# Two scan steps and two attention groups in one loop turn of a conv, state-space, attention and expert kernel

## The chip, the core and the metric

The kernel runs on one core of a Trainium2 chip. The metric is device microseconds of one execution. The kernel before takes 5496.23 us, the median of 3 runs (5489.41 to 5500.91).

The engines are named as in the profile: PE is TensorE (matrix products, accumulated in PSUM banks), DVE is VectorE, ACT is ScalarE, POOL is GpSimd, and SP is the queue that issues nearly all transfers. Each works through its own instructions strictly in program order.

## The reference

An image batch `x` (4, 128, 64, 64) goes through two layers. Layer 0 is group norm, a depthwise convolution with a pointwise one, and a state-space scan (Mamba) on four channel chunks. Layer 1 is attention over 4096 tokens with 4 heads of 32, then the two best of 8 experts. The change touches the scan and the attention:

```python
# scan, for every channel d, state n (16 of them), step t
h = dA_t * h + dBu_t              # dA = exp(delta * A), dBu = delta * B * xin
y = jnp.einsum('bdn,bn->bd', h, C_t)

# attention
scores = jnp.einsum('bhnd,bhmd->bhnm', q, k) * scale
att = jax.nn.softmax(scores, axis=-1)
out = jnp.einsum('bhnm,bhmd->bhnd', att, v)
```

## The kernel before, in words

**Tiling.** An image of 4096 positions is cut into 8 blocks of 512 (`BLK`). The scan of a block runs for two chunk pairs `p`, each on 128 partitions, and for 16 states `n`. One (batch, block, pair, state) is a *unit*; there are 4 x 8 x 2 x 16 = 1024. Attention is cut into *groups*: for one head and 1024 queries, two tiles of 128 keys. There are 1024 groups.

**The loop.** The order of instructions is written out by hand. The main loop takes one turn, a *slot*, per unit, and goes on afterwards until the remaining groups and expert work are done. In a slot:

- SP fetches the B and C rows of the unit three slots ahead from DRAM (`rows<-bcd`, broadcast over the partitions, 4 buffers).
- ACT copies the last column of the unit before into `states`, and computes `da`, the exponential of the decay, for the unit two slots ahead.
- PE computes the scores of the next group: four matmuls into two PSUM tiles `sc` of two banks each. The pool of `sc` has two buffers, so one group fills it. ACT turns them into `pT` by two exponentials.
- DVE runs the unit: `h` = B row times `du`, then the scan (`tensor_tensor_scan`) with the saved state as start value, then `hc` = C row times `h`.
- From `ALONE` (unit 128) on, POOL adds the `hc` of every odd state to that of the even one, and PE adds four transposes of the sum to the PSUM tile `y`, from two slots after the odd state on. Before `ALONE`, PE adds each `hc` by a full matmul with the identity one slot later. After the last state, `y` is copied out, turned back by four transposes, and goes on (`summed_up`).
- PE computes the weighted sums `av` of the group of the slot before (`weighted`, four matmuls in two passes each). When a sum is complete, ACT copies it from PSUM (`avs`), which has one buffer.

**Side work.** All else (norms, convolution, projections, softplus, routing, experts) is written as generators in two lanes, X and Y, of which `advance` runs one stage at a time: each lane has one call marked second and one marked first per slot. Stages hand on from one engine to another: PE writes a PSUM tile, DVE or ACT reads it in a later call. In a slot the calls come after the scan step and the score matmuls: X second, Y first, then the transposes of `y`, Y second, then `weighted`, X first. `until` runs stages early where a unit's inputs aren't ready.

**Transfers.** `send` puts a transfer in a list that `flush` issues at the start of a later slot. Keys and values of the next part are fetched three groups before a part ends.

Of the kernel before, what the change touches and what calls it, by code (L numbers as in the profile page):

```python
# [9 lines left out]
F32 = mybir.dt.float32  # L10
F32R = mybir.dt.float32r
# [25 lines left out]
def conv_mamba_attn_moe_kernel(ctx: ExitStack, tc: tile.TileContext, t: dict):  # L37
# [450 lines left out]
        return ps_work.tile(shape or [P, BLK], F32, tag=f"work{lane}", name=f"ps_{lane}")  # L488

    def tmp(lane, name, shape=None):  # L490
        return side.tile(shape or [P, BLK], F32, tag=f"tmp{lane}", name=name, bufs=4)

    def transposed(lane, src):
        ps = work(lane)
# [184 lines left out]
    def inputs(b, i, p):  # L679

        xn, pairs = xn_of[b, i], pairs_of[b, i]
        r = slice(DI * p, DI * p + DI)
        while held:
            yield
            yield
        held.add("in")
        ps = work("Y")
        summed(ps, [(inxc[:, j, :], pairs[:, p, 2 * j : 2 * j + BLK]) for j in range(2)])
        pz = work("X")
        mm(pz, inz[r, :], xn[r, 3 : 3 + BLK])  # L690
        yield
        xin = mix.tile([P, BLK], F32, name="xin", bufs=2)
        scalar.activation(xin, ps, AF.Silu, bias=cb)
        zs = mix.tile([P, BLK], F32, name="zs", bufs=4)
        scalar.activation(zs, pz, AF.Silu)
        yield

        pb = work("X")
        mm(pb[0:DI, :], wbc, xin)
        ps = work("Y")  # L700
        mm(ps, wdt, xin)
        yield
        held.clear()
        bc = tmp("Y", "bc")[0:DI, :]
        scalar.copy(bc, pb[0:DI, :])
        bcd = dram.tile([2, NST, 2 * BLK], F32, name="bcd", bufs=4)
        send(bcd.rearrange("c n (k q) -> (c n k) q", k=2), bc)

        e = tmp("Y", "e")
        scalar.activation(e, ps, AF.Abs, bias=dtb)  # L710
        scalar.activation(e, e, AF.Exp, scale=-1.0)
        ln = tmp("Y", "ln")
        scalar.activation(ln, e, AF.Ln, bias=1.0)
        delta = mix.tile([P, BLK], F32, name="delta", bufs=2)
        scalar.activation(delta, ps, AF.Relu, bias=dtb)
        yield
        yield

        du = mix.tile([P, BLK], F32, name="du", bufs=2)
        lost = du  # L720
        gpsimd.tensor_scalar(lost, e, 1.0, -1.0, ALU.add, ALU.add)
        gpsimd.tensor_sub(lost, e, lost)
        gpsimd.tensor_add(ln, ln, lost)
        gpsimd.tensor_add(delta, delta, ln)
        gpsimd.tensor_mul(du, delta, xin)
        in_of[b, i, p] = xin, zs, delta, du, bcd
        done.add(("in", b, i, p))
        yield

    states = [mix.tile([P, 2, NST], F32, name=f"state{k}") for k in range(2)]  # L730

    def fetched(b, i, p, n):

        bcd = in_of[b, i, p][4]
        w = mix.tile([P, 2, BLK], F32, name="rows", bufs=4)
        sync.dma_start(
            out=w.rearrange("p k q -> p (k q)"),
            in_=bcd[:, n, :][None].to_broadcast([DI, 2, 2 * BLK]),
        )
        return w  # L740

    def decayed(b, i, p, n):
        da = mix.tile([P, BLK], F32, name="da", bufs=3)
        scalar.activation(da, in_of[b, i, p][2], AF.Exp, scale=amat[:, n : n + 1])
        return da

    def scan(b, i, p, n, w, da):

        du = in_of[b, i, p][3]
        h = mix.tile([P, BLK], F32, name="h", bufs=3)  # L750
        vector.tensor_mul(h, w[:, 0, :], du)
        vector.tensor_tensor_scan(
            out=h, data0=da, data1=h, initial=0.0 if i == 0 else states[b % 2][:, p, n : n + 1],
            op0=ALU.mult, op1=ALU.add,
        )
        hc = mix.tile([P, BLK], F32, name="hc", bufs=5)
        vector.tensor_mul(hc, w[:, 1, :], h)
        return h, hc

    def scanned(b, i, p, y):  # L760
        xin, zs, delta, du, bcd = in_of.pop((b, i, p))
# [28 lines left out]
    def closed(b, i):  # L790
# [58 lines left out]
        for d, w, bias in ((kd, wkn, bkn), (qd, wqn, bqn)):  # L849
            ps = work("X")  # L850
            mm(ps, w, xa)
            yield
            hi = side.tile([P, BLK], F32R, name="hi", bufs=2)
            vector.tensor_scalar(hi, ps, bias, None, ALU.add)
            lo = side.tile([P, BLK], F32R, name="lo", bufs=2)
            vector.scalar_tensor_tensor(
                lo, ps, bias, hi.bitcast(F32), ALU.add, ALU.subtract
            )
            for half, w in enumerate((hi, lo)):
                w = w.bitcast(F32)  # L860
                if len(d.shape) == 4:
                    send(d[:, :, half, sj], w[:, None, :].to_broadcast([P, 2, BLK]))
                else:
# [54 lines left out]
    def attention(b):  # L918
# [25 lines left out]
        for at, part in enumerate(parts):  # L944
# [9 lines left out]
            for g in range(0, NT * n, STEP):  # L954
# [5 lines left out]
                if g >= NT * n - 3 * STEP and ahead is None and at + 1 < len(parts):  # L960
                    nxt = parts[at + 1]
                    if ready(b, nxt):
                        ahead = load(nxt, qs if nxt[:2] == (q, h) and not nxt[5] else None)
                pTs = []
                for j in range(g, g + STEP):
                    sc = ps_sc.tile([P, 2, BLK], F32, name="sc")
                    for u in range(2):
# [1 line left out]
                            sc[:, u, :], ks[:, j * P : (j + 1) * P],  # L969
                            qs[:, u * BLK : (u + 1) * BLK],  # L970
                        )
                    pT = att.tile([P, 2, BLK], F32, name="pT", bufs=4)
                    scalar.activation(pT, sc, AF.Exp, scale=ATT_SCALE)
                    pTs.append((v[:, j // NT, j % NT, :], pT))
                yield (
                    b, q, h, pTs, first and g == 0, last and g + STEP == NT * n, prev, final,
                )

    sums, partial, total, inverse, later = [None], {}, {}, {}, deque()

    def weighted(group):
        b, q, h, pTs, first, last, prev, final = group
# [175 lines left out]
    def advance(lane, second):  # L1158
# [3 lines left out]
        while True:  # L1162
            if lane not in running:

                tasks = lanes[lane] if lanes[lane] or slot < len(units) else lanes["X"]
                if not tasks or not all(k in done for k in tasks[0][2]):
                    return False

                if (
                    tasks[0][0][0] == "out" and slot < len(units) + 4  # L1170
                    and not 2 <= slot % (2 * NST) < NST + 2
                ):
                    return False
# [62 lines left out]
        left.clear()  # L1236

    groups = attention_groups()
    units = [(b, i, p, n) for b, i in blocks for p in range(2) for n in range(NST)]

    ALONE = NB // 2 * 2 * NST
    rows, decays, old, due, closing = {}, {}, None, deque(), deque()
    even, y_of, waiting, slot = None, {}, None, 0
    while slot < len(units) or due or closing or waiting or left or later or lanes["X"] or running:
        flush()

        for ahead in range(slot if slot == 0 else slot + 3, min(slot + 4, len(units))):
            until(("in", *units[ahead][:3]))
            rows[ahead] = fetched(*units[ahead])
        if old:  # L1250
            (b, i, p, n), h = old
            if i < NB - 1:
                scalar.copy(states[b % 2][:, p, n : n + 1], h[:, BLK - 1 : BLK])
            old = None
        for ahead in range(slot if slot == 0 else slot + 2, min(slot + 3, len(units))):
            decays[ahead] = decayed(*units[ahead])
        group = next(groups, None)
        if slot < len(units):
            unit = units[slot]
            h, hc = scan(*unit, rows.pop(slot), decays.pop(slot))  # L1260
            old = unit, h
            b, i, p, n = unit

            if slot < ALONE:
                due.append((slot + 1, unit, hc, n == 0))
            elif n % 2 == 0:
                even = hc
            else:
                gpsimd.tensor_add(even, even, hc)
                due.append((slot + 2, unit, even, n == 1))  # L1270
        advance("X", True)
        advance("Y", False)
        while closing and closing[0][0] <= slot:
            turned_back(*closing.popleft()[1:])
        while due and due[0][0] <= slot:
            at, unit, term, first = due.popleft()
            b, i, p, n = unit
            if first:
                y_of[b, i, p] = ps_y.tile([P, BLK], F32, name="y")
            y, ends = y_of[b, i, p], n == NST - 1  # L1280
            if at <= ALONE:
                mm(y, ident, term, first, ends)
                if ends:
                    summed_up(b, i, p, y_of.pop((b, i, p)))
            else:
                turned_on(y, term, first, ends)
                if ends:
                    yT = mix.tile([P, BLK], F32, name="yT")
                    scalar.copy(yT, y_of.pop((b, i, p)))
                    closing.append((slot + 1, b, i, p, yT))  # L1290
        advance("Y", True)
        if waiting:
            weighted(waiting)
        waiting = group
        advance("X", False)
        while later and later[0][0] <= slot:
            next(later.popleft()[1])
# [28 lines left out]
def _laid_out(i):  # L1326
# [15 lines left out]
    z = np.zeros((P, P), np.float32)  # L1342
    inx, inz = z.copy(), z.copy()
    wout = np.zeros((P, 2, P), np.float32)
    wbc = np.zeros((P, 2, NST, 2), np.float32)
    xdt, dtT = np.zeros((4, P), np.float32), np.zeros((4, P), np.float32)
    for c in range(2):
        d = slice(c, P, 2)
# [3 lines left out]
            inz[s, d] = c0["in_proj_w"][DI:].T  # L1352
            wout[d, p, s] = c0["out_proj_w"].T

        wbc[d, c] = c0["x_proj_w"][2:].reshape(2, NST, DI).transpose(2, 1, 0)
        xdt[2 * c : 2 * c + 2, d] = c0["x_proj_w"][:2]
        dtT[2 * c : 2 * c + 2, d] = c0["dt_proj_w"].T

# [53 lines left out]
```

## Time and profile before

| | us |
|---|---|
| median of 3 runs | 5496.23 |
| the profiled execution | 5490.03 |
| its span, first to last instruction | 5488.3 |
| ACT `pT`, 2048 exponentials | 1983.1 |
| PE `av`, 8192 passes | 2022.7 |
| DVE scans with a start value, 896 | 1364.1 |
| PE `sc`, 4096 | 1333.3 |
| DVE `hc`, 1024 | 882.4 |
| DVE `h` (multiplication), 1024 | 843.3 |
| ACT `da`, 1024 | 751.2 |
| POOL `hc`, 448 additions | 677.6 |
| ACT table loads, 320 | 410.6 |

The busy time of a group counts moments in which one of its instructions runs; the groups of one engine follow each other, and those of different engines overlap. All recorded instructions carry line 445, that of a helper that orders them, so groups are told apart by their tiles: `h<-rows,du` is the multiplication, `h<-da,state,h` the scan, `hc<-rows,h` the reading on DVE, `hc<-hc` the addition on POOL, `sc<-qs,ks` the scores, `av<-pT,v` the weighted sums, `y<-ident,hc` the transposes.

### The profile page before, as it was taken

The numbers are of one execution on the slowest core, as the hardware profiler recorded it, in microseconds if no ns is written. First come the engines' busy times: TensorE is split into PE (matmuls) and PEld (weight loads), VectorE is DVE, ScalarE is ACT, GpSimd is POOL, SyncE is SP. The second block draws the span as 40 slices with busy tenths as digits, with TensorE's granted clock in tenths as the row PEclk, the third lists the DMA queues.
The fourth block names the chain that finished last, engine by engine and source line by source line (L and its number), as shares of the span: only waits on it lengthen the run. The fifth ranks groups of instructions, "written<-read, shape, count | busy, mean of one in ns | idle before, by whom it ended". The sixth has DMA issues, their size and how long they took to land.

```text
span 5488.3 us, 63616 instructions
## 1 busy us (share of the span) xinstructions
PE 4780.5 (87%) x18986; PEld 2159.0 (39%) x18986; DVE 4404.5 (80%) x6659; ACT 3923.3 (71%) x6045; POOL 1981.4 (36%) x1533
## 2 busy tenths in 40 slices
PE   4677798898988888898898898888889898999997
PEld 2223343443444443444444443344444443444443
DVE  4898888889888889988988888888989888871231
ACT  3455687788877777677877777777777777766553
POOL 2222345445433344344533434343443334420100
PEclk8778998999999999999999999999999999999998
DMA  3556566677656667666765666667765666765542
GB/s 98 173 178 195 194 216 229 223 233 254 219 197 206 226 206 244 221 225 220 252 214 196 221 209 233 237 202 240 250 207 200 209 225 196 249 200 167 168 148 68
DMA packets 451714, 1131.67 MB, mean 206 GB/s; under 512 B 51985, under 2 KB 135330, under 8 KB 451362
## 3 DMA queue, kind: packets, MB, share of 16 engines
q1 hardware_dynamic: 450194, 1126.74, 61.5%
q8 instruction: 153, 2.51, 0.2%
q14 instruction: 199, 1.63, 0.1%
q10 hardware_dynamic: 1168, 0.80, 0.1%
HBM read 967.12 MB, written 143.39 MB: 202 GB/s over the span
## 4 chain that ended last, share of the span: by engine, by line
PE 41%; DVE 31%; ACT 11%; issue 8%; DMA 7%; POOL 1%; SPq 0%; DVEq 0%; ACTq 0%; POOLq 0%
DVE h L445 17%; PE av L445 16%; PE sc L445 10%; PE ps_X L445 8%; PE ps_Y L445 5%; ACT pT L445 4%; DVE hc L445 3%; DMA ks<-kd 2%; PE y L445 2%; ACT xt L445 2%; DVE cm L445 2%; ACT L445 2%; DMA rows<-bcd 1%; DVE share L445 1%; DMA inv<-inverse 1%
## 5 line engine op out<-in xcount | busy, mean ns | idle before, releaser
L445 ACT ACTIVATE pT<-sc 128x1024 f32<-128x1024 f32 x2048 | 1983.1, 1022 | 976.0 <-PE sc L445 973.0
L445 PE MATMUL av<-pT,v 128*64 128x512 f32 x8192 | 2022.7, 615 | 7.3 <-ACT avs L445 7.1
L445 DVE TENSOR_TENSOR_SCAN h<-da,state,h 128x512 f32<-128x512 f32 x896 | 1364.1, 1522 | 100.7 <-ACT da L445 8.1
L445 PE MATMUL sc<-qs,ks 128*128 128x512 f32 x4096 | 1333.3, 447 | 116.1 <-ACT pT L445 60.1
L445 POOL TENSOR_TENSOR hc<-hc 128x512 f32<-128x512 f32 x448 | 677.6, 1513 | 1526.0 <-DVE hc L445 1354.4
L445 PEld LDWEIGHTS sc<-qs,ks 128*128 128x128 f32 x4096 | 728.1, 196 | 808.7 <-ACT pT L445 297.1
L445 DVE TENSOR_TENSOR hc<-rows,h 128x512 f32<-128x512 f32 x1024 | 882.4, 862 | 79.9 <-DVE h L445 2.7
L445 DVE TENSOR_TENSOR h<-rows,du 128x512 f32<-128x512 f32 x1024 | 843.3, 824 | 42.5 <-POOL du L445 25.6
L445 PEld LDWEIGHTS av<-pT,v 128*64 128x64 f32 x8192 | 506.0, 138 | 913.5 <-issue 880.9
L445 ACT ACTIVATE da<-delta,amat 128x512 f32<-128x512 f32 x1024 | 751.2, 734 | 16.7 <-DVE h L445 12.6
L445 ACT ACT_TABLE_LOAD x319 | 409.3, 1283 | 18.6 <-PE ps_Y L445 13.3
L445 POOL TENSOR_TENSOR rsY<-rsY,mhalf 128x4 f32<-128x4 f32 x100 | 139.9, 1399 | 575.1 <-DVE shiftY L445 574.1
L445 ACT COPY state<-h 128x1 f32<-128x1 f32 x896 | 177.2, 198 | 221.8 <-DVE h L445 221.4
L445 POOL TENSOR_TENSOR avs<-avs,prev 128x512 f32<-128x512 f32 x96 | 145.1, 1511 | 425.3 <-ACT avs L445 343.3
L445 PE MATMUL y<-ident,hc 128*128 128x128 f32 x1792 | 274.9, 277 | 7.0 <-POOL hc L445 7.0
L445 PEld LDWEIGHTS y<-ident,hc 128*128 128x128 f32 x1792 | 223.1, 142 | 106.4 <-issue 50.4
L445 DVE TENSOR_TENSOR share<-share,xf 128x1024 f32<-128x1024 f32 x128 | 174.5, 1363 | 105.0 <-DMA share<-sharesX 73.9
L445 PE MATMUL ps_X<-share,w_ew 128*128 128x512 f32 x432 | 224.4, 643 | 39.4 <-DVE share L445 39.4
L445 POOL TENSOR_TENSOR rsX<-rsX,mhalf 128x4 f32<-128x4 f32 x92 | 112.3, 1221 | 304.7 <-DVE shiftX L445 304.3
L445 POOL TENSOR_SCALAR du<-e 128x512 f32<-128x512 f32 x64 | 128.3, 2005 | 251.5 <-ACT e L445 251.5
L445 POOL TENSOR_TENSOR zs<-xin,zs 128x512 f32<-128x512 f32 x64 | 107.4, 1678 | 290.1 <-DVE xin L445 280.9
L445 PE MATMUL y<-hc,ident 128*128 128x512 f32 x256 | 169.4, 758 | 45.5 <-DVE hc L445 45.3
(239 smaller groups left out, 4832.2 us busy)
## 6 DMA issues: line engine op xcount, KB each, us to landing
rows<-bcd SPq DMA_DIRECT2D x1024, 512.0 KB
ks<-kd SPq DMA_DIRECT2D x192, 512.0 KB
qs<-qd SPq DMA_DIRECT2D x161, 512.0 KB
share<-sharesX SPq DMA_DIRECT2D x108, 512.0 KB
v<-vd SPq DMA_DIRECT2D x192, 256.0 KB
ks<-kd SPq DMA_DIRECT2D x128, 256.0 KB
avd<-avs SPq DMA_DIRECT2D x96, 256.0 KB
prev<-avd SPq DMA_DIRECT2D x96, 256.0 KB
```

Source lines behind the costliest of these rows:

```text
L445: return lambda *args, **kw: queued(op(*args, **kw))
```

## The change

A turn of the loop now takes two units (states `n` and `n+1`) and two groups, called A and B here, in two halves.

- The DRAM layout of B and C is changed, so that one transfer brings the B rows of both states, and another the C rows of both.
- `h`, `da` and `hc` become tiles for two states. `h` and `da` have one extra column between the two states: `da` is 0 there and `h` holds the start value of the second state, so that one scan over 1025 columns runs both.
- DVE has three instructions a turn: `driven` (1024 columns, `du` broadcast), `scan` (1025), `read` (1024).
- ACT copies the start value of the second state into `h` (`carried`), also for the first block, and two last columns into `states` at once (`kept`). `kept` stands in the second half, in front of group B's exponentials. `da` is computed one turn ahead, in two tiles kept for the whole run.
- Scores are still computed by `attention_groups`; the exponentials move to `exponentials`. In the first half come A's scores and exponentials, the transposes of `y`, and then `weighted` for B of the turn before and for A. In the second half come B's scores and exponentials; B's weighted sums wait for the next turn.
- POOL adds the two halves of `hc` after `read`; the transposes come in the first half of the next turn, behind A's scores. Units before `ALONE` are added by transposes too (two terms a turn), and `ALONE` is now reached at unit 64 instead of 128 (`slot` still counts units).
- Each lane has four calls a turn. In the first half: X second before the scores and `driven`; Y first before the exponentials, the transposes and `scan`; Y second and X first before the `weighted` pair. In the second half: X second before `read` and the scores; Y first, Y second, X first after them.
- The temporaries of lane X get 6 buffers instead of 4, and `hi` and `lo` are taken from them.

```diff
-    def decayed(b, i, p, n):
-        da = mix.tile([P, BLK], F32, name="da", bufs=3)
-        scalar.activation(da, in_of[b, i, p][2], AF.Exp, scale=amat[:, n : n + 1])
-        return da
+    decays = [mix.tile([P, 2, BLK + 1], F32, name=f"da{k}") for k in range(2)]
+    for k in range(2):
+        gpsimd.memset(decays[k][:, 0, BLK:], 0.0)
...
+    def carried(unit):
+        b, i, p, n = unit
+        if (i, p, n) == (0, 0, 0):
+            gpsimd.memset(states[b % 2], 0.0)
+        h = mix.tile([P, 2, BLK + 1], F32, name="h", bufs=2)
+        scalar.copy(h[:, 0, BLK:], states[b % 2][:, p, n + 1 : n + 2])
+        return h
+
+    def kept(unit, h):
+        b, i, p, n = unit
+        if i < NB - 1:
+            scalar.copy(states[b % 2][:, p, n : n + 2], h[:, :, BLK - 1])
+
+    def driven(unit, h, w):
+        b, i, p, n = unit
         du = in_of[b, i, p][3]
-        h = mix.tile([P, BLK], F32, name="h", bufs=3)
-        vector.tensor_mul(h, w[:, 0, :], du)
+        vector.tensor_mul(h[:, :, 0:BLK], w, du[:, None, :].to_broadcast([P, 2, BLK]))
+
+    def scan(unit, h, da):
+        b, i, p, n = unit
+        h, da = (a.rearrange("p k q -> p (k q)")[:, 0 : 2 * BLK + 1] for a in (h, da))
         vector.tensor_tensor_scan(
-            out=h, data0=da, data1=h, initial=0.0 if i == 0 else states[b % 2][:, p, n : n + 1],
+            out=h, data0=da, data1=h, initial=states[b % 2][:, p, n : n + 1],
             op0=ALU.mult, op1=ALU.add,
         )
-        hc = mix.tile([P, BLK], F32, name="hc", bufs=5)
-        vector.tensor_mul(hc, w[:, 1, :], h)
-        return h, hc
+
+    def read(h, w):
+        hc = mix.tile([P, 2, BLK], F32, name="hc", bufs=2)
+        vector.tensor_mul(hc, w, h[:, :, 0:BLK])
+        return hc
...
+    def exponentials(group):
+        pTs = []
+        for v, sc in group[3]:
+            pT = att.tile([P, 2, BLK], F32, name="pT", bufs=4)
+            scalar.activation(pT, sc, AF.Exp, scale=ATT_SCALE)
+            pTs.append((v, pT))
+        return *group[:3], pTs, *group[4:]
...
+        at = slot // 2
         flush()
+        fetch((at + 1, 1))
+        unit = units[at] if at < len(units) else None
+        advance("X", True)
         group = next(groups, None)
+        if unit:
+            h = h_of.pop(at)
+            driven(unit, h, rows.pop((at, 0)))
+        advance("Y", False)
+        here = [pending] if pending else []
+        pending = None
+        if group:
+            here.append(exponentials(group))
+        while due and due[0][0] <= at:
...
+                turned_on(y, term, n == 0 and k == 0, ends and k == len(terms) - 1)
...
+        if unit:
+            scan(unit, h, decays[at % 2])
+        advance("Y", True)
+        advance("X", False)
+        prepared(at + 1)
+        for each in here:
+            weighted(each)
...
+        slot += 1
+        flush()
+        fetch((at + 2, 0))
+        advance("X", True)
+        if unit:
+            hc = read(h, rows.pop((at, 1)))
             if slot < ALONE:
+                due.append((at + 1, unit, [hc[:, 0, :], hc[:, 1, :]]))
             else:
+                gpsimd.tensor_add(hc[:, 0, :], hc[:, 0, :], hc[:, 1, :])
+                due.append((at + 1, unit, [hc[:, 0, :]]))
+            kept(unit, h)
+        group = next(groups, None)
+        if group:
+            pending = exponentials(group)
         advance("Y", False)
+        while closing:
+            turned_back(*closing.popleft())
         advance("Y", True)
         advance("X", False)
```

`prepared(at + 1)` calls `decayed` and `carried` for the next turn's unit; `turned_on` is the four transposes into `y`, `turned_back` the four that turn a finished `y` around.

## The prediction

> **What bounds the kernel now.** I read the busy shares first, with the chain of work that ended last, then the page's forty slices.
>
> ```profile
> PE 4780.5 (87%) x18986; PEld 2159.0 (39%) x18986; DVE 4404.5 (80%) x6659; ACT 3923.3 (71%) x6045; POOL 1981.4 (36%) x1533
> PE 41%; DVE 31%; ACT 11%; issue 8%; DMA 7%; POOL 1%; SPq 0%; DVEq 0%; ACTq 0%; POOLq 0%
> PE   4677798898988888898898898888889898999997
> DVE  4898888889888889988988888888989888871231
> ```
>
> TensorE (PE) and VectorE (DVE) are both nearly full, and the chain hops between them. The slices show three stages: at first DVE is full and PE not, then both are, and in the last four PE is alone. Cut there (100, 690 and 4900 us), the windows of all engines give each stage (columns: stretch, length, then busy us of PE, PEld, DVE, ACT, POOL, the granted clock and the DMA share):
>
> ```profile
> 100.00:690.00 590.00, 434.89 (x1158) 178.35 (x1160) 511.60 (x739) 336.56 (x610) 170.27 (x140) 0.81 0.55 184
> 690.00:4900.00 4210.00, 3762.42 (x15556) 1724.23 (x15552) 3717.76 (x5368) 3252.39 (x5013) 1752.32 (x1308) 0.96 0.67 222
> 4900.00:5488.00 588.00, 543.42 (x2164) 237.38 (x2160) 148.36 (x423) 307.42 (x380) 40.66 (x43) 0.95 0.41 135
> ```
>
> Windows of tile h hold 458, 2612 and 0 DVE instructions on h, three to a step: 153, 871 and 0 steps, so 76, 435 and 0 of the new turns. The windows of sc (four matmuls a group) hold 34, 856 and 134 groups, 67 new turns in the last stage. In the middle PE idles 4210 - 3762 = 448 us. For what, the waits of PE in that window say (total, times, longest):
>
> ```profile
> PE ps_X L445 <- DVE aT L445: 75.6, 21, 5.6
> PE ps_X L445 <- DVE prX L445: 65.4, 18, 4.6
> PE sc L445 <- ACT pT L445: 57.8, 84, 3.4
> PE y L445 <- POOL hc L445: 3.1, 2, 2.7
> ```
>
> With share 39.4, lo 31.7, cm 12.7 and 9.6, and gmv 12.2, PE waits 247 us for DVE: side work (lanes X and Y) whose DVE half stands behind a scan. Two waits that the change touches are small: scores for an exponential, 58 us, and the transposes of y for POOL's addition, 3 us.
>
> **DVE, wide instructions.** Durations per shape (minimum/median/maximum in ns), first h, then share, which is a 1024-wide multiplication by a broadcast operand, like the new ones:
>
> ```profile
> L445 DVE TENSOR_TENSOR h<-rows,du x1024: 621/684/1784, 96.7 to 4894.9; 128x512 f32<-128x512 f32 x171
> L445 DVE TENSOR_TENSOR_SCAN h<-da,state,h x896: 1282/1284/2395, 201.2 to 4895.7; 128x512 f32<-128x512 f32 x180
> L445 DVE TENSOR_TENSOR share<-share,xf x128: 1211/1221/2001, 1426.9 to 5479.7; 128x1024 f32<-128x1024 f32 x128
> ```
>
> Two narrow multiplications are 2 x 684 = 1368 ns, a wide one 1221: 0.147 us of fixed cost saved, and there are two such pairs a turn. No row shows a 1025-wide scan. Its bounds are twice the narrow one, 2.57 us, and that less the same fixed cost, 2.42; I take 2.42, since scan and multiplication start and end alike. In DVE's side-free run around 310 us the steps follow at 2.785 us, 0.125 more than the three durations; one such gap goes. A turn saves 0.29 + 0.15 + 0.125 = 0.57 us of 5.57.
>
> First stage: 76 turns x 0.57 x DVE's busy share there, 511.6/590 = 0.87: **-38** (0 to -43). The transposes that replace full matmuls there (0.53 us per four, as at 3011.89 below) lie on PE, idle 155 us. But `ALONE` now ends at unit 64 instead of 128, so POOL adds in 32 turns where it didn't; a scan beside an addition took 2.10 us (at 3027.31) instead of 1.28: 32 x 0.82 x 0.87 = **+23** (0 to 26).
>
> Middle stage: what counts is what PE no longer waits. Before, every side operation on DVE stands behind the whole step of 2.8 us. After, in half one the Y lane's first call stands behind the wide multiplication alone (1.2 us), and in half two the X lane's second call stands before the reading multiplication. About half the calls lose the DVE work ahead of them, and for the rest it shrinks by a tenth (0.57 of 5.57); so I take 0.55 of the 247: **-136** (0 to -247).
>
> **TensorE, the order.** The timeline in a stretch without side work (start, duration, what), then one with a late exponential:
>
> ```profile
> 3007.85 1.21 PE L445 MATMUL sc<-qs,ks 128*128 128x512 f32 x4
> 3009.00 1.94 PE L445 MATMUL av<-pT,v 128*64 128x512 f32 x8
> 3010.86 1.19 PE L445 MATMUL sc<-qs,ks 128*128 128x512 f32 x4
> 3011.89 0.60 PE L445 MATMUL y<-ident,hc 128*128 128x128 f32 x4
> 3012.42 1.94 PE L445 MATMUL av<-pT,v 128*64 128x512 f32 x8
> 3014.29 1.19 PE L445 MATMUL sc<-qs,ks 128*128 128x512 f32 x4
> ...
> 3039.77 1.92 ACT L445 ACTIVATE pT<-sc 128x1024 f32<-128x1024 f32 x2
> 3040.83 0.73 PE L445 MATMUL sc<-qs,ks 128*128 128x512 f32 x2 [3.31 <-ACT pT L445]
> 3041.75 1.19 PE L445 MATMUL sc<-qs,ks 128*128 128x512 f32 x2 [0.18 <-ACT pT L445]
> ```
>
> Two steps cost PE 6.44 us: 1.15 + 1.86 + 1.03 + 0.53 + 1.87. A score group in front of av costs 1.15, in front of anything else 1.03. The turn has only the latter: 1.03 + 0.53 + 1.87 + 1.87 + 1.03 = 6.33, 0.11 less; x (435 + 67) = **-55** (0 to -55).
>
> **The score buffers.** Scores have two buffers, one group fills both, and each is free when its exponential ends. Before, av (1.9 us) stands between two score groups and covers that. After, both av stand together, so group B's scores and the next turn's group A follow each other, with only four of the eight lane calls between. The exponentials begin 0.84 us after the scores (3007.85 to 3008.69 in ACT's timeline) and two take 1.94, so B's end 2.78 us after its start; the last lines show PE going on some 0.06 us later, and half a group is 0.52. The next group thus ends 3.36 us after B's start, without the wait 2.06: a loss of 1.30 us less the side work between. Program order with this trace's durations (1.0 us per 512-wide matmul in two passes, 0.22 per transpose, 0.3 per 128-wide matmul) puts no work in 176 of 512 such places, 0.95 us on average in 152, and more than 1.30 in 184: (176 x 1.30 + 152 x 0.35)/512 = 0.55 us a turn, 0.51 in the middle, 0.83 at the end, where less side work stands. 435 x 0.51 = **+222** and 67 x 0.83 = **+56** (0 to 278). Where a side operation itself waits in such a place, that wait fills it too; this touches only the 152 partly filled ones, 54 us in all, of which I take half off: **-25**.
>
> **Tighter waits.** POOL adds the two halves of hc, and PE transposes the sum. Before, the transposes stand a slot or more later: the addition that began at 3704.66 was used at 3713.35. After, they follow the next turn's first scores. If both engines begin a turn together, PE gets there after its busy time per turn, 3762/435 = 8.65, less 0.11, plus 0.51, plus the scores' 1.03: 10.1 us. DVE's read ends after 3718/435 - 0.57 = 8.0 less the side calls behind it (three of eight, of 2.1 us): 7.2. Slack 2.9; an addition takes 1.57 (median), and is covered until POOL has something else in hand: the softplus chain on e, ln, delta and du, 2.0 + 1.7 + 1.7 + 1.6 + 1.7 = 8.7 us by the page's groups, 64 times, half of them ahead of an addition. One that starts 0.6 us into the turn gives 0.6 + 8.7 + 1.57 = 10.9, 0.8 late. Bounds: 0, and 1.57 x 435 = 683 if the read ends as PE arrives; I take 32 x 0.8 = **+25**, nearer to today's 3. Behind a late addition stand both av groups on PE. On ACT, group B's exponentials now stand behind the copies of the state, which wait for this turn's scan; ACT waited 81 us for h in the middle (0 to 81), and B's exponentials have no slack: **+20**.
>
> [...]
>
> **Nothing.** The row transfers keep count (1024) and size and are asked for one to two turns ahead (before, three steps); DVE waited 2.5 us for them in all. They are cover lost only if DMA, at 0.67, fills up. SP's other transfers queue behind them as before, each waiting for the buffer that DVE released. Table loads stay at 320. The 64 more state copies are 0.2 us each on ACT (71% busy). The keys are asked for three groups ahead as before.
>
> **Sum** against the profiled execution's own 5490.03 us (span 5488.3; the median of the runs, 5496.23, is 6 above): -38 + 23 - 136 - 55 + 222 + 56 - 25 + 25 + 20 = +92, so 5582; I give 5580.
>
> **Rivals.** *DVE leads* (faster). Much of PE's idle time comes from DVE, whose work shrinks by a tenth. If three quarters of the 247 go (-185) and half of the score waits lie where PE would have waited for DVE anyway (139), then 5490 - 38 + 23 - 185 - 55 + 139 = 5374. For it: DVE is as full as PE, and scan and multiplication hold a fifth of the chain. Against it: in 176 turns there is nothing between the score groups, so nothing else hides the wait. It decides once fewer than half of them show. *The addition locks PE to DVE* (slower still): if DVE runs late by more than the 2.9 - 1.57 = 1.3 us left over, each turn waits at the transposes, say 0.6 us: 435 x 0.6 = 261 in place of 25, about 5820. Against it: DVE has 0.57 us more air a turn. *It doesn't do what it says*: the wide scan costs two narrow ones and the waits are hidden: 5490 + 56 - 55, no change. The program order does show 511 runs of two av groups in a row, none with a change of sums inside.
>
> **How the numbers follow.** Forecast 0.43 (5500 to 5720 by its own terms), DVE leads 0.39, lock 0.13, nothing 0.05. Faster or slower means over 0.2%, 11 us, about what a measurement of this kernel tells from no change: faster 0.39, same 0.05, slower 0.56. The range runs from 5345, a little under the faster rival, to 5745; what it leaves out is the far half of the lock and gains in which nearly all 247 us go.
>
> **What would show it.** Right: PE waits for sc behind pT of 200 us or more, in half-microsecond pieces; wide multiplications of 1.22 and scans of 2.42 us; av in runs of 16; PE's waits for aT, prX and share about halved; the last stage 50 us longer. Wrong: sc behind pT still under 100 us (the faster rival), or PE's y behind POOL's hc in the hundreds (the lock).

## The result, and the profile after

The changed kernel takes 6009.7 us (median of 4 runs, 6001.27 to 6011.26), the kernel before 5498.51 in the same comparison: a ratio of 1.093 (95% interval 1.0917 to 1.0943), 511 us more. The sign of the forecast was right; its size (5580) and its range (to 5745) were not. The profiled execution took 6001.27 us, its span is 5999.5.

The busy shares of the changed kernel, its chain of waits, and two of the rows in forty slices:

```profile
PE 4871.7 (81%) x19146; PEld 2234.3 (37%) x19146; DVE 3913.8 (65%) x5123; ACT 3940.5 (66%) x6117; POOL 2289.7 (38%) x1571
PE 43%; DVE 15%; ACT 14%; POOL 12%; issue 8%; DMA 6%; SPq 1%; DVEq 0%; POOLq 0%; ACTq 0%
PE   4546787887888888888888888888888888899997
DVE  4877666766677767776777777776667777661221
```

VectorE did get shorter work: 3914 us busy instead of 4405, and its share of the chain is halved (31% to 15%). But the program did not shrink with it: PE is at 81% instead of 87%, and POOL, which had 1% of the chain, has 12%. Where this happens, the windows of the three stages say (columns as before; the scans end at about 5353 us, before at 4897):

```profile
100.00:705.00 605.00, 348.09 (x1230) 187.06 (x1230) 455.77 (x492) 317.91 (x591) 258.37 (x167) 0.72 0.52 173
705.00:5360.00 4655.00, 3928.46 (x15670) 1785.08 (x15668) 3284.81 (x4080) 3293.01 (x5109) 1973.94 (x1316) 0.94 0.60 202
5360.00:5999.00 639.00, 555.66 (x2138) 243.12 (x2134) 146.50 (x423) 302.75 (x376) 39.11 (x43) 0.94 0.37 123
```

By the windows of h and sc they hold 74, 438 and 0 turns, and 28, 864 and 132 groups. A turn of the middle stage takes 4655/438 = 10.63 us; two steps took 4210/435 = 9.68. That is 0.95 x 438 = 416 of the 511 us. No stage is faster: the first takes 605/74 = 8.2 us a turn instead of 590/76 = 7.8, the last 639/132 = 4.84 us a group instead of 588/134 = 4.39.

PE idles 1128 us (5999.5 - 4871.7), before 708. Its waits in the middle stage (total, times, longest):

```profile
PE y L445 <- POOL hc L445: 228.2, 103, 6.5
PE sc L445 <- ACT pT L445: 195.3, 510, 4.1
PE av L445 <- ACT pT L445: 68.6, 29, 3.1
PE ps_X L445 <- DVE prX L445: 45.1, 19, 2.7
```

The first row was 3.1 us before. The prediction had named it: "y behind POOL's hc in the hundreds (the lock)" was to show the forecast wrong. All of PE's waits in the whole span, summed by the engine that ended them, stand against the prediction's terms like this (us):

| | before | after | difference | terms of the prediction |
|---|---|---|---|---|
| PE waits for exponentials (`pT`) | 60 | 318 | +258 | +222 + 56 - 25 = +253, and +20 (`kept`) |
| PE waits for DVE | 361 | 227 | -135 | -136 |
| PE waits for POOL's `hc` | 7 | 302 | **+295** | **+25** |
| PE waits for other results of ACT | 182 | 236 | +54 | 0 |
| PE waits for DMA | 77 | 36 | -41 | 0 |
| PE busy | 4780.5 | 4871.7 | **+91** | **-55** |

The rows for waits add up to about +430, of which the span shows +420 as idle time. Two rows look right, to 15 us and to 1, and two are far off. What each of these waits was worth in time, the experiments show.

The DVE durations of the changed kernel, per shape (minimum/median/maximum in ns), are as estimated, 1.22 and just under 2.42 us:

```profile
L445 DVE TENSOR_TENSOR h<-rows,du x512: 1208/1220/2351, 96.9 to 5348.3; 128x1024 f32<-128x1024 f32 x171
L445 DVE TENSOR_TENSOR_SCAN h<-da,state,h x512: 2282/2355/3349, 98.2 to 5349.6; 128x1025 f32<-128x1025 f32 x171
```

The timeline of the changed kernel in a turn without side work on PE (start, duration, what, and in brackets the idle time before it with what ended it):

```profile
3302.79 1.20 PE L445 MATMUL sc<-qs,ks 128*128 128x512 f32 x4
3304.70 0.73 PE L445 MATMUL sc<-qs,ks 128*128 128x512 f32 x2 [0.71 <-ACT pT L445]
3305.61 0.73 PE L445 MATMUL sc<-qs,ks 128*128 128x512 f32 x2 [0.18 <-ACT pT L445]
3306.18 0.60 PE L445 MATMUL y<-ident,hc 128*128 128x128 f32 x4
3306.71 3.65 PE L445 MATMUL av<-pT,v 128*64 128x512 f32 x16
3310.30 1.20 PE L445 MATMUL sc<-qs,ks 128*128 128x512 f32 x4
```

Group B's scores at 3302.79 and the next A's at 3304.70 stand together, and the second pair waits for two exponentials in turn. The turn takes 3310.30 - 3302.79 = 7.51 us. Two steps took 6.44, and the prediction's own terms give 6.44 - 0.11 + 1.30 = 7.63. So the price of one bare place was right.

Here is what a late addition costs, in the timelines of POOL and PE:

```profile
2306.67 2.15 POOL L445 TENSOR_TENSOR delta<-delta,ln 128x512 f32<-128x512 f32 x1
2308.90 3.14 POOL L445 TENSOR_TENSOR du<-delta,xin 128x512 f32<-128x512 f32 x1
2311.99 1.71 POOL L445 TENSOR_TENSOR avs<-avs,prev 128x512 f32<-128x512 f32 x1
2313.66 1.71 POOL L445 TENSOR_TENSOR hc<-hc 128x512 f32<-128x512 f32 x1
2315.42 1.11 PE L445 MATMUL y<-ident,hc 128*128 128x128 f32 x4 [6.52 <-POOL hc L445]
```

The addition stands behind the rest of the softplus chain and an addition of sums. PE stands still for 6.52 us, with both av groups queued behind. The four transposes then take 1.11 us, not 0.60.

### The profile page after: what moved, and what is told of

Read it like the earlier page. It is cut to its first block, busy times and chain, and to the rows that moved or that the text cites. A ratio compares the mean times of both kernels' runs of the same rounds, so it can differ in the third digit from the quotient of the medians.

```text
span 5999.5 us, 61840 instructions
## 1 busy us (share of the span) xinstructions
PE 4871.7 (81%) x19146; PEld 2234.3 (37%) x19146; DVE 3913.8 (65%) x5123; ACT 3940.5 (66%) x6117; POOL 2289.7 (38%) x1571
## 4 chain that ended last, share of the span: by engine, by line
PE 43%; DVE 15%; ACT 14%; POOL 12%; issue 8%; DMA 6%; SPq 1%; DVEq 0%; POOLq 0%; ACTq 0%
PE av L445 21%; PE ps_X L445 8%; PE sc L445 7%; DVE h L445 6%; ACT pT L445 6%; PE ps_Y L445 5%; ACT L445 3%; POOL du L445 3%; PE y L445 2%; POOL hc L445 2%; DMA inv<-inverse 2%; POOL ln L445 2%; DVE hc L445 1%; POOL rsY L445 1%; ACT xt L445 1%
## 5 line engine op out<-in xcount | busy, mean ns | idle before, releaser
L445 DVE TENSOR_TENSOR_SCAN h<-da,state,h 128x1025 f32<-128x1025 f32 x512 | 1359.2, 2655 | 197.7 <-ACT h L445 150.4
L445 PEld LDWEIGHTS av<-pT,v 128*64 128x64 f32 x8192 | 575.7, 146 | 1223.7 <-issue 1032.3
L445 DVE TENSOR_TENSOR h<-rows,du 128x1024 f32<-128x1024 f32 x512 | 705.3, 1378 | 38.5 <-POOL du L445 25.4
L445 DVE TENSOR_TENSOR hc<-rows,h 128x1024 f32<-128x1024 f32 x512 | 692.3, 1352 | 46.0 <-DVE h L445 15.4
L445 PE MATMUL y<-ident,hc 128*128 128x128 f32 x2176 | 387.9, 311 | 351.1 <-POOL hc L445 301.7
L445 PEld LDWEIGHTS y<-ident,hc 128*128 128x128 f32 x2176 | 296.1, 159 | 521.1 <-POOL hc L445 364.4
L445 ACT COPY avs<-av 128x512 f32<-128x512 f32 x160 | 94.2, 589 | 372.1 <-PE av L445 321.6
L445 ACT COPY state<-h 128x2 f32<-128x2 f32 x448 | 89.1, 199 | 266.8 <-DVE h L445 263.3
L445 ACT ACTIVATE xt<-ps_Y,shiftY,rsY 128x128 f32<-128x128 f32 x380 | 143.1, 460 | 139.9 <-POOL shiftY L445 131.8
L445 DVE BATCH_NORM_STATS2 stY<-ps_Y 128x6 f32<-128x128 f32 x380 | 84.3, 284 | 216.1 <-PE ps_Y L445 215.8
```

What stands on the lines that cost most here:

```text
L445: return lambda *args, **kw: queued(op(*args, **kw))
```

## The experiments

All times are medians, with the ratio to the kernel before and its 95% interval. The kernel before lay between 5496.1 and 5498.7 in every comparison. The table is a way back from the changed kernel, one edit after another; only e8 takes an earlier one back, the later place of the transposes, and puts its own in its stead.

| kernel | us | ratio | step |
|---|---|---|---|
| changed | 6009.7 | 1.093 [1.0917, 1.0943] | |
| e2: scores and sums unpaired | 5849.6 | 1.0643 [1.0625, 1.0661] | -160 |
| e3: and transposes later in the turn | 5739.9 | 1.0444 [1.0427, 1.0461] | -110 |
| e5: and state copies at the turn's end | 5740.9 | 1.0435 [1.0413, 1.0457] | +1 |
| e8: transposes two turns behind the addition (in e2's order) | 5653.0 | 1.0278 [1.0254, 1.0302] | -88 |
| e10: and narrow DVE instructions | 5567.2 | 1.0124 [1.0108, 1.0139] | -86 |
| e12: and additions from step 128 only | 5556.6 | 1.0108 [1.0091, 1.0125] | -11 |

**e1, the transposes behind the weighted sums.** If the addition is late by less than the av pair lasts, moving the transposes behind it hides the wait.

```diff
-        while due and due[0][0] <= at:
-            ...
         if unit:
             scan(unit, h, decays[at % 2])
...
         for each in here:
             weighted(each)
+        while due and due[0][0] <= at:
+            ...
```

> The changed kernel with one thing moved: the transposes of y stand behind the pair of weighted sums instead of in front of it, 3.7 us later in TensorE's queue. Theory L (the lock: TensorE stands at the transposes until POOL has added, 302 + 48 us of waits): these waits fall below 60 us and the time to about 5750 (6010 less some 260). Theory S (the score buffers: two score groups in a row with two buffers, 249 us of waits): TensorE only trades one wait for another, 5930 to 6010. Theory R (wide DVE instructions block POOL and so all side work is late): 5950 to 6010, with POOL's busy time still near 2290.

Measured: 5832.7 us, ratio 1.0611 [1.0593, 1.0629], 177 less than the changed kernel. PE's waits for POOL's hc fall from 302 to 57 us, its waits for exponentials stay (318 to 335). So 177 us of the time hung on the transposes standing in front of the weighted sums while the addition was late.

**e2, pairing undone.** A's weighted sums move to the second half, behind B's scores, so that an av group stands between any two score groups.

```diff
-        pending = None
+        pending = held_a = None
         if group:
-            here.append(exponentials(group))
+            held_a = exponentials(group)
...
             pending = exponentials(group)
+        if held_a:
+            weighted(held_a)
```

> The changed kernel with the pair of weighted sums taken apart again: group A's follow group B's scores in the second half, so that one group of weighted sums stands between any two score groups. DVE's wide instructions stay. Theory S: waits of sc for pT fall from 249 to under 80 us and the time by 200 to 250, to 5760 to 5810. Theory L: the waits at the transposes stay at 300 us or more, the time moves by less than 80 (5930 or more). Theory R: 5930 or more.

Measured: 5849.6 us, 160 less. PE's waits for pT are halved (318 to 151), those for the addition nearly stay (302 to 275).

**e3, both.**

> Both edits together: transposes behind group B's weighted sums, group A's weighted sums behind B's scores. If L and S together are the whole loss, about 5500 (6010 less 260 less 240), with DVE's saving perhaps under that, 5400. Theory R: it stays above 5700, because DVE's wide instructions are still there.

Measured: 5739.9 us, 270 less than the changed kernel where the two alone add up to 177 + 160 = 337. The two waits overlap in part. With 242 us still missing, something else was at work. PE's waits for DVE, 227 us in the changed kernel, are back at 307.

**e4, pairing alone, in the kernel before.** Nothing else of the change is in it: no wide instructions, the transposes and additions as before.

```diff
-        if waiting:
-            weighted(waiting)
-        waiting = group
+        if slot % 2 == 0:
+            waiting = [group]
+        else:
+            for each in (waiting or []) + [group]:
+                if each:
+                    weighted(each)
+            waiting = None
```

> The kernel before with nothing but the pair: no weighted sums in even slots, in odd slots those of the slot before and of this slot, one behind the other. DVE's narrow steps and the late transposes stay. Theory S: sc waits for pT by 200 us more than in the kernel before, and the time rises by 200 to 280, to 5700 to 5780. Theory L: POOL's addition keeps its slack, so within 80 of 5500. Theory R: within 80 of 5500.

Measured: 5934.4 us, ratio 1.0799 [1.0781, 1.0817]: 436 us lost by pairing alone. Three of its waits (of PE and ACT):

```profile
ACT avs L445 <- PE av L445: 300.3, 127, 4.4
PE sc L445 <- ACT pT L445: 221.2, 496, 4.4
PE av L445 <- ACT pT L445: 94.2, 30, 4.3
```

PE's waits for pT rise from 60 to 315 us, as in the changed kernel. Pairing exposes an exponential twice: the score groups wait for their buffers, and av of the newer group may wait for the exponential it has just ordered. ACT loses too: its copies of finished sums wait 300 us for the long av pair (64 before), and ACT's side results stand in order behind them. PE's waits for other results of ACT rise from 182 to 356 us, and PE itself is busy for 90 us more (4870), at a mean granted clock of 0.923 instead of 0.940.

**e5, the state copies.** ACT waited 370 us for h in e3, more than for anything but PE's scores. The edit is in e3.

```diff
-            kept(unit, h)
...
         advance("Y", True)
         advance("X", False)
+        if unit:
+            kept(unit, h)
```

> As e3_both (5740), and the copies of the last columns into the states (kept) moved from in front of group B's exponentials to the end of the turn. Theory K (ACT stands at kept until the scan ends, 370 us of waits, and the exponentials behind it come late): waits of ACT state for DVE h fall below 100, of sc for pT from 158 below 80, the time by 100 to 200, to 5540 to 5640. Theory N (the wide DVE instructions cost: they block POOL and put side work behind longer instructions): within 60 of 5740. Theory G (POOL's addition still stands too close before the transposes): within 60 of 5740.

Measured: 5740.9 us, no change, although ACT's wait for h falls from 370 to 88 us. PE's waits for exponentials did fall, from 158 to 126 us, but those for DVE rose by 35. The time didn't hang on that wait.

**e6, the DVE half of the change undone, in e3.** The loop, the tiles and the transfers stay; only the instructions are narrow. `carried` loses its copy, since the second scan can start from `states`.

```diff
-        scalar.copy(h[:, 0, BLK:], states[b % 2][:, p, n + 1 : n + 2])
...
-        vector.tensor_mul(h[:, :, 0:BLK], w, du[:, None, :].to_broadcast([P, 2, BLK]))
+        for k in range(2):
+            vector.tensor_mul(h[:, k, 0:BLK], w[:, k, :], du)
...
-        vector.tensor_tensor_scan(
-            out=h, data0=da, data1=h, initial=states[b % 2][:, p, n : n + 1],
+        for k in range(2):
+            vector.tensor_tensor_scan(
+                out=h[:, k, 0:BLK], data0=da[:, k, 0:BLK], data1=h[:, k, 0:BLK],
+                initial=states[b % 2][:, p, n + k : n + k + 1],
...
-        vector.tensor_mul(hc, w, h[:, :, 0:BLK])
+        for k in range(2):
+            vector.tensor_mul(hc[:, k, :], w[:, k, :], h[:, k, 0:BLK])
```

> As e3_both, with the three wide DVE instructions cut into six narrow ones in the same places (two multiplications, two scans, two readings), and without the copy of the second state's start value, which narrow scans don't need. Theory N: POOL's busy time falls from 2270 to about 2000, its waits for shift halve, and the time falls by 100 to 200 although DVE has 290 us more to do, to 5540 to 5640. Theory K: the lost saving shows, 5740 to 5900, since ACT's waits for the scan get longer. Theory G: 5740 to 5850.

Measured: 5622.9 us, ratio 1.022 [1.0202, 1.0239], **117 less than e3**, with DVE busy for 172 us more (3932 to 4105). What gets shorter is POOL, 2269 to 2086 us busy, though not its long operations: the means of the softplus chain's five add up to 9.5 us in both.

**e7, narrow and late state copies.**

> Both edits of e5_kept_late and e6_narrow on e3_both. If K and N are together the rest of the loss, 5450 to 5550. If wide instructions are a gain, slower than e5_kept_late by up to 290 times the half that lies on the path, some 145 us.

Measured: 5624.0 us, ratio 1.023 [1.0212, 1.0248], the same as e6. The copies cost nothing here either.

**e8, a whole turn more for the addition.** The edit is in e2 with the state copies late; lane X gives up one buffer for the third `hc`.

```diff
-        hc = mix.tile([P, 2, BLK], F32, name="hc", bufs=2)
+        hc = mix.tile([P, 2, BLK], F32, name="hc", bufs=3)
...
-                due.append((at + 1, unit, [hc[:, 0, :], hc[:, 1, :]]))
+                due.append((at + 2, unit, [hc[:, 0, :], hc[:, 1, :]]))
...
-                due.append((at + 1, unit, [hc[:, 0, :]]))
+                due.append((at + 2, unit, [hc[:, 0, :]]))
```

> As e5_kept_late, but the transposes stand at the changed kernel's place, in front of the weighted sums, and use the additions of two turns before (a third hc buffer, lane X's temporaries 5 instead of 6 to make room). Theory G: waits at the transposes for POOL hc, 87 us in e3_both, fall below 15 and the time by 60 or more below e5_kept_late. Otherwise within 30 of e5_kept_late.

Measured: 5653.0 us, 88 less than e5. PE's waits for the addition fall from 91 to 28 us, while those for other results of ACT rise by 59 and those for DMA by 54. Against e2 it is 197 less, for a step that the prediction priced at 25.

**e9, only the scan narrow, in e3.** `carried`'s copy goes with it; the multiplications stay wide.

> e3_both with the scan alone cut back into two of 512 columns (and so without the copy of the second state that the 1025-column scan needs); both multiplications stay 1024 wide. e6_narrow cut all three and gained 117 us on e3_both (5739.9 to 5622.9). Theory 'scan and its copy': the gain comes from the 2.3 us scan in one piece and from the copy that the scan waits for (ACT's copy cost DVE 113 us of waits in e3_both), so this run gives about 5625. Theory 'wide multiplications': the gain comes from 1.2 us multiplications that hold up POOL's small operations (their means fell from 1.9 to 1.4 us in e6_narrow), so it stays at 5720 to 5745, with POOL's rsX still near 1.9 us. Between 5660 and 5700 both have a part.

Measured: 5661.3 us, ratio 1.0292 [1.0278, 1.0306], 79 less than e3 and 38 more than e6: scan and copy give two thirds of e6's gain, the multiplications one third. Nothing but the multiplications differs between e9 and e6, so these 38 us are the price of their width. POOL's small operations (128x4, minimum/median/maximum in ns) show what the width does to them. First e3, all wide:

```profile
L445 POOL TENSOR_TENSOR rsX<-rsX,mhalf x92: 1007/2006/2078, 44.9 to 5685.4; 128x4 f32<-128x4 f32 x92
L445 POOL TENSOR_TENSOR shiftY<-shiftY,rsY x100: 199/1497/1851, 39.6 to 5684.2; 128x4 f32<-128x4 f32 x100
```

Then e9, wide multiplications and narrow scans:

```profile
L445 POOL TENSOR_TENSOR rsX<-rsX,mhalf x92: 1006/2005/2017, 46.2 to 5605.4; 128x4 f32<-128x4 f32 x92
L445 POOL TENSOR_TENSOR shiftY<-shiftY,rsY x100: 198/427/442, 41.0 to 5604.2; 128x4 f32<-128x4 f32 x100
```

Then e6, all narrow:

```profile
L445 POOL TENSOR_TENSOR rsX<-rsX,mhalf x92: 1006/1472/1483, 46.0 to 5591.8; 128x4 f32<-128x4 f32 x92
L445 POOL TENSOR_TENSOR shiftY<-shiftY,rsY x100: 198/835/850, 40.8 to 5590.6; 128x4 f32<-128x4 f32 x100
```

rsX takes 1.01 us at least, 2.01 typically beside 1.22 us multiplications, 1.47 beside those of 0.68. shiftY takes 0.2 us at least, 1.5 typically with the scan of 2.3 us, and 0.4 to 0.8 without it. What rsX takes beyond its least is close to 1.0 and 0.5 us, where the multiplications differ by 0.54. The timeline of e3 shows a scan and a shiftY beside it:

```profile
2043.51 2.35 DVE L445 TENSOR_TENSOR_SCAN h<-da,state,h 128x1025 f32<-128x1025 f32 x1
2044.36 1.50 POOL L445 TENSOR_TENSOR shiftY<-shiftY,rsY 128x4 f32<-128x4 f32 x1
```

shiftY begins 0.85 us into the scan and ends with it. All 62 shiftY of e3 that begin during a scan end within 20 ns of the scan's end, and so do all 61 of e9 and all 62 of e6. In e6 they begin only 0.43 us into a narrow scan, in e9 0.85, which is why they are the longer ones in e6. So these operations of POOL are lengthened by what is left of the DVE instruction beside them, and a wide one has more left.

By which path this becomes time is shown in part only: ACT waits for shiftY for 238 us in e3, 175 in e9 and 167 in e6 (81 in the kernel before), and matrix products of PE stand behind ACT. Whether e9's 79 us come from the scan's width or from the copy that DVE waited 113 us for isn't told apart: both went. But without the copy DVE waits some 85 us in e9 and 84 in e6 for `da`, which ACT makes at the same place, so most of the 113 us did not go with the copy.

**e10, everything so far in one kernel: e8 with narrow instructions.**

> e8_turn_later (scores unpaired, transposes two turns behind the addition, state copies late) with all three wide DVE steps of a turn cut into two of 512 columns. If the width costs by itself, its 117 us come on top of e8's gain: 5653 - 117 = 5536, some 40 above the kernel before. If the narrow steps gained only because the addition came earlier for the transposes, which here have a whole turn of slack already, the gain is gone: 5630 to 5655.

Measured: 5567.2 us, 86 less than e8, between the two expectations: most of the width's price stands. That the missing quarter is slack that e8 had already given is likely, but not shown.

**e11, narrow instructions alone, in the changed kernel.**

> The changed kernel with only the three wide DVE steps cut into two of 512 columns each (no copy of the second state); scores stay paired and the transposes stay where they are. If the width costs the same 117 us as beside e3_both: 6010 - 117 = 5893. If it mainly makes the addition late for the transposes (POOL hc, 302 us of PE's waits in the changed kernel), more: 5800 or below, with those waits under 150. If PE's waits for the exponentials hide it, 5970 to 6010.

Measured: 5885.5 us, ratio 1.07 [1.0685, 1.0714], 124 less than the changed kernel. PE's waits for the addition fall only from 302 to 263, so the gain is not this wait alone: PE idles 61 us less in all (1066), and is busy for 50 less (4822).

**e12, the first stage as long as before, in e10.**

```diff
-    ALONE = NB // 2 * NST
+    ALONE = NB // 2 * 2 * NST
```

> e10_later_narrow with the first stage as long as in the kernel before: POOL adds the two halves of hc only from scan step 128 on instead of from 64 (`ALONE` doubled). e10_later_narrow is 69 us above the kernel before, and what it lacks it lacks early: from 2800 us on it handles as many score groups as before, but by then it is some 65 us behind. If POOL's additions between steps 64 and 128 are what holds the first stage up (the prediction put them at +23; POOL is busy 245 us in 100 to 700 against 178), this run gives 5525 to 5545, and POOL is again near 180 us busy there. If the first stage is held up by something else (y transposes, order of the side calls, PE at a lower granted clock), it stays at 5555 to 5580.

Measured: 5556.6 us, 11 less than e10; the two intervals [1.0108, 1.0139] and [1.0091, 1.0125] overlap. So the 32 turns with additions cost little here, where an addition has two turns. No version beats the kernel before.

## Why the prediction was wrong

**The step that failed** is "Tighter waits". It took the late addition for 32 turns of 0.8 us, +25; PE waited 295 us more for it, and e1, which takes most of these waits away, gains 177. The step's mechanism holds: the addition "is covered until POOL has something else in hand". In 56 of the 103 waits of the middle stage, 172 of the 228 us, the addition follows directly on other work of POOL. In 24 this is the end of the softplus chain, with 97 us of waiting, 4.0 each instead of 0.8. In 18 it is an addition of sums (avs), 52 us, and in 14 shiftX, 22 us; both were left out of the step. In the other 47, 56 us, POOL stood idle before the addition, so its input came late. Two inputs of the step were off. The chain was costed at 8.7 us with the durations of before; after, the means of its five operations add up to 9.8, above all by 2.39 (ln) and 2.11 us (du from delta), 1.74 and 1.69 before. And the slack of 2.9 us was a mean over all turns: a turn without side work lasts 7.51 us on PE, where the step reckoned with 9.05 (8.65 - 0.11 + 0.51), so that PE arrives 1.5 us earlier. Whether these two make up all of the 3.2 us that a wait is longer than foreseen is not shown.

**The rival that came true in part** is "the addition locks PE to DVE", given 0.13 and about 5820. The place was right; the cause was for the most part not DVE but POOL's queue (172 of the 228 us).

**POOL beside DVE.** The rows of e3 and e6 show rsX stretched by 1.0 us with wide multiplications and by 0.5 with narrow ones. All 60 shiftY of the changed kernel that begin during a scan end within 20 ns of its end, as those of e3, e6 and e9 do. The additions of hc in the changed kernel take longer beside DVE too:

```profile
383.73 1.22 DVE L445 TENSOR_TENSOR h<-rows,du 128x1024 f32<-128x1024 f32 x1
383.95 2.11 POOL L445 TENSOR_TENSOR hc<-hc 128x512 f32<-128x512 f32 x1 [5.00 <-DVE hc L445]
```

Of the 480 additions, 205 have no DVE instruction beside them and take 1.27 us in the median; the 87 that begin during a wide multiplication `h` take 2.14. The prediction's +25 reckoned with 1.57 for each, the median of before. But the measured 295 us are not mainly this: with narrow instructions in e11, 263 of the 302 us of waits remain. Most of them come from the queue in front of the addition (172 of 228 us in the middle stage).

**-136, DVE's side work.** The size was right, the conclusion was not. In the middle stage the seven rows fell from 247 to 115 us, but unevenly: aT from 76 to 13, prX from 65 to 45, share from 39 to 35, so the rule of one half is not what the rows show. Over the whole span PE waited 135 us less for DVE while it waited 550 us more elsewhere. When some of those waits are taken away, waits for DVE come back: 307 us in e3, 293 in e12, against 361 before. A late engine hides that another one is late. And here is the second step that failed, "DVE, wide instructions" (0.57 us saved a turn): the shorter DVE work (-491 us busy) was no gain in itself. Of the forecast, -38 and some -12 (a tenth of half of the 247) were for the width alone. E6, e10 and e11 do the same steps in narrow instructions, with 172 to 196 us more DVE time, and are 117, 86 and 124 us faster. The step left out what a wide instruction, with the copy that the wide scan needs, does to the other engines.

**+253, the score buffers.** PE's waits for pT rose by 258, and the last stage lost 0.45 x 132 = 60 us against +56. Both agreements are partly luck. Of the 258 us, 69 are waits of av, which the step didn't have; those of sc rose by 189. In the last stage PE waits for pT for 40 us, and e2, without pairs, still takes 605/132 = 4.58 us a group there instead of 4.39. As a price of pairing in the kernel before, the term was too low: 436 us in e4, since the step counted only PE's score buffers, not av behind a fresh exponential, nor ACT held by the copies of sums. In the changed kernel e2 gets back 160, beside e1's edit 93 (5832.7 to 5739.9), probably because the other waits lie in the same turns.

**-55, PE's order.** A bare turn is right to 0.12 us, but PE is 91 us busier. Its granted clock fell from a mean of 0.940 to 0.913. The trace has it at 0.50 from 2311.34 to 2318.17 us, in and after the 6.52 us wait: the fall came 2.4 us into the wait, which began at 2308.90, and the four transposes behind it took 1.11 us instead of 0.60. In the middle stage all 19 waits of PE of 4 us or more end at 0.50, and 10 of the 21 of 3 to 4 us. Over all transposes of y that read hc the mean rose from 277 to 311 ns: the 498 that start at 0.50 take 421 in the median, the others 272. So these long waits are paid twice, which the sum left out. The late additions are not the only cause of the busier PE: e4 has hardly any (2 us of waits), and PE is 90 us busier there too.

**+20, `kept`.** Nothing by e5 and e7. **-38 and +23, the first stage.** No gain to be seen (8.2 us a turn instead of 7.8): PE waits there for POOL's additions, 73.5 us where it was 3.9, and for hc from DVE, 48 us where it was 45. Of the 73.5 us, 36 belong to additions before which POOL stood idle. E12 puts the additions of the 32 turns at some 11 us with two turns for each; in the changed kernel, with one, their price wasn't measured.

**What stays open.** E12 has left of the change the loop of two halves with its order of the side calls, the transposes in place of full matmuls in the first stage, the lane buffers and the wider transfers; it is 1.0108 [1.0091, 1.0125] of the time before, some 60 us. From 2800 to 4200 us e10 handles as many score groups as the kernel before (564 and 560 exponentials), up to 1400 somewhat fewer (358 and 368), from 1400 to 2800 clearly fewer (536 and 566). What is lost is lost before 2800 us, most of it behind the first stage. The waits of PE that grew in e10 are those for other results of ACT (182 to 317 us) and for DMA (77 to 116); which of the moved calls makes them wasn't tried.

## What to carry to other kernels

Before an instruction is widened to save its fixed cost, look at which other engine works beside it, and at what the instruction will hold up: here wide instructions, with 172 to 196 us less VectorE work, made the kernel slower than the same steps in narrow pieces. When a result is used sooner than before, count everything that can stand ahead of its producer in that engine's queue, in the worst turns and not in the mean one. And a wait removed from a trace is worth its size only if the same turns have no other late engine behind it: in e5, 282 us less of ACT's waits for h brought nothing.

## What was not expected of the hardware

The stretching goes both ways: beside POOL's du of 3.14 us at 2308.90 (typically 1.7), the scan that DVE began at 2307.78 took 3.20 us. Of the 512 wide scans, the 213 with no POOL instruction beside them take 2.28 to 2.36 us, the 299 with one 3.17 in the median; over all, the mean is 2.65 us against a median of 2.36. And one scan over 1025 columns saves little: 2.28 us at least, against twice 1.21 in e6 (1.28 in the kernel before).
